# Layer 3's second mix: second half of the features first, later tokens first, and the next weights' contraction swapped to match

## The chip, the cores and the metric

The kernel runs on one NeuronCore of a Trainium2 chip. What counts is the device time of one execution in microseconds (us). The kernel before was run three times: 2449.55, 2449.95 and 2450.09 us, a median of 2449.95 us.

## What is computed

The input `x` has 128 graphs of 64 nodes with 256 features (8192 tokens), and all graphs share one 64 x 64 adjacency `adj`. Four layers follow one another, each added to `x`: a graph convolution with LSTMs over windows of nodes, masked attention, a graph convolution with batch normalisation, and layer 3, which this case is about. All of it is fp32. Layer 3, cut to what matters:

```python
def _slconv(x, adj, S, W):                 # here S is adj too
    support = jnp.einsum('bnf,fh->bnh', x, W)
    return jnp.einsum('nm,bmh->bnh', adj * S, support)
h = jnp.maximum(_layernorm(x), 0.0)
h = relu(_slconv(h, adj, adj, W1))         # 256 -> 512 features
h = relu(_slconv(h, adj, adj, W2))         # 512 -> 1024
x = x + _slconv(h, adj, adj, W3)           # 1024 -> 256
```

Mixing over nodes and multiplying with weights can be exchanged, so the kernel does for each group of tokens: mix, W1, Relu, mix, W2, Relu, W3, mix, add.

## The kernel before

**Groups.** The tokens are cut into 16 groups (`NG`) of 512 (`GN`), each of 4 token tiles (`GT`) of 128 tokens, which are two graphs. Layer 3 is one loop over `g` from 0 to 16 (lines 1571 to 1614). A pass issues, in program order: `first_weights` of group g; `last_mix` (k = 0) of group g - 1; `second_mix` of group g; `last_mix` (k = 1) and `finish` of group g - 1; `second_weights` of g; `start` (layer norm and first mix) of g + 1; `third_weights` of g. In group 0 there is no `last_mix`, and other matmuls (transposes back to tokens, line 1301) stand in that place.

**The order of the work.** The kernel is written in a framework whose planner puts each engine's instructions in order, by program order and by its own reckoning of what is ready, and sets the waits. Each engine then works through its queue in that order. `issue_after` adds an order within an engine. PSUM tiles are all taken from one pool of eight banks (`bank`, line 49).

**Mix** (line 132). It multiplies by the 64 x 64 matrix `w2s`. For two feature chunks of 128 at a time (`c0`, `c0 + 1`) and each token tile `t` it does 8 matmuls on 64 x 64 quarters of the array (line 144), with the activations as the stationary operand. Each is two records in the profile[...]. The results lie in two banks, one for each graph of a tile; a copy on VectorE and one on ScalarE (line 154) bring them to SBUF. The second mix has four chunks: chunks 0 and 1 with all four tiles, then chunks 2 and 3.

**The weights as seven products.** Every multiplication with weights is cut into 2 x 2 blocks and done as seven block products in place of eight (`seven`, line 170; `sevens`, line 241). The products 1, 5, 6 and 7 come first, into four banks in this order. ScalarE copies 1 and 5 to SBUF (lines 179 and 180), VectorE adds 6 and 7 to them (182 and 183). Then `finish`:
- Block (1,1) is summed on GpSimd from SBUF (line 187); its Relu is on ScalarE (line 237).
- Product 2 goes into the first bank; block (0,0) is its Relu (line 234).
- Product 3 goes into the second bank; block (0,1) is a sum on VectorE (line 193), then a Relu (237).
- Product 4 goes into the fourth bank; block (1,0) is a sum on VectorE (line 197), then a Relu (237).

In `first_weights` (line 1408, matmuls at 1418) a block (m, n) holds the tokens of tiles 2m and 2m + 1 and the feature chunks 2n and 2n + 1. Its last block, (1,0), is handled in two parts, one for each token tile (`parts` of line 1429).

**Second weights** (line 1438, matmuls at 1454). Blocks of the mixed activations `m1`: `act[c][n]` has chunks 2c and 2c + 1 and half n of the token columns. `differences` makes four combinations of them on VectorE (line 214). The weights' blocks `a2` and sums `s2s` are made once, on GpSimd, in `layer3_weights` (line 1154).

**Last mix and finish** (lines 1517 and 1530). `last_mix` does 4 matmuls for each k into two banks `pss`; `finish` adds the banks to `x` on VectorE (line 1542) and sends `x` out.

Of the kernel before, what the change touches and what calls it, by code (L numbers as in the profile page):

```python
# [9 lines left out]
AF = mybir.ActivationFunctionType  # L10
# [4 lines left out]
P = 128  # L15
D = 256
NODES = 64
NTOK = 8192
GT = 4
GN = GT * P  # L20
NG = NTOK // GN
# [17 lines left out]
def adj_preln_kernel(ctx: ExitStack, tc: tile.TileContext, x_in, adj, vec, bg0, bg1,  # L39
# [9 lines left out]
    def bank(shape=(P, 512)):  # L49
        return psp.tile(list(shape), F32, tag="ps", name="ps")  # L50
# [22 lines left out]
    w2s = const.tile([P, NODES], F32, tag="w2s", name="w2s")  # L73
# [55 lines left out]
                )  # L129
        return pss  # L130

    def mix(src, a2, chunks, dst, copies, swap=False, banks=None, behind=lambda t, last: None):

        for c0 in range(0, chunks, 2):
            pss = banks or [bank((P, 2, GT, NODES)) for _ in range(2)]
            for t in range(GT):
                for c in range(2):
                    for half in range(2):  # L140
                        for b in range(2):
                            rows = slice(b * 64, b * 64 + 64)
                            col = (c0 + c) * P + half * 64
                            last = nc.tensor.matmul(  # L144
                                pss[b][half * 64 : half * 64 + 64, c, t, :],
                                lhsT=src[rows, t, col : col + 64],
                                rhs=a2[rows, :],
                                start=True, stop=True,
                            )
                behind(t, last.ins)  # L150
            for b in range(2):
                if swap:
                    to = dst[:, c0 : c0 + 2, :].rearrange("p c (k b m) -> p b c k m", b=2, m=P)
                    last = copies[b](to[:, b], pss[b].rearrange("p c (k q) n -> p c k (q n)", q=2))
                else:
                    to = dst[:, c0 : c0 + 2, :].rearrange("p c (t b n) -> p b c t n", b=2, n=NODES)
                    last = copies[b](to[:, b], pss[b])
        return last.ins

    on_vector, on_scalar = nc.vector.tensor_copy, nc.scalar.copy  # L160
# [993 lines left out]
    def layer3_weights():  # L1154

        w31_tile = arena(keep)
        w31 = w31_tile[:, 0:2, :]
        nc.sync.dma_start(out=w31, in_=l3w1.rearrange("(c p) f -> p c f", p=P))  # L1160
        w32 = [arena(ar_left), arena(ar_left)]
        w32_view = l3w2.rearrange("(c p) (k f) -> k p c f", p=P, k=2)
        for k in range(2):
            nc.sync.dma_start(out=w32[k], in_=w32_view[k])
        w33 = arena(ar_left).rearrange("p a (b f) -> p (a b) f", f=D)
        nc.sync.dma_start(out=w33, in_=l3w3.rearrange("(c p) f -> p c f", p=P))
        a2 = [[w32[m][:, 2 * c : 2 * c + 2, :] for c in range(2)] for m in range(2)]
        s2s = [t[:, i : i + 2, :] for t in (arena(ar_left), arena(ar_left)) for i in (0, 2)]
        sums(nc.gpsimd, *a2[0], *a2[1], *s2s)
        nc.gpsimd.tensor_scalar(a2[1][1], a2[1][1], -1.0, None, ALU.mult)  # L1170
        b1 = [[w31[:, c, n * D : (n + 1) * D] for n in range(2)] for c in range(2)]
        t1s = [w31_tile[:, 2 + i // 2, (i % 2) * D : (i % 2 + 1) * D] for i in range(4)]
        differences(nc.gpsimd, *b1[0], *b1[1], *t1s, negate=True)
        b3 = [[w33[:, 4 * c : 4 * c + 4, n * P : (n + 1) * P] for n in range(2)] for c in range(2)]

        t3s = [t[:, i, :].rearrange("p (c f) -> p c f", c=4) for t in (a2[1][0], w1) for i in range(2)]
        differences(nc.gpsimd, *b3[0], *b3[1], *t3s, negate=True)
        return b1, t1s, a2, s2s, b3, t3s
# [175 lines left out]
    def first_start():  # L1354

        a = arena(ar_left)
        h = a[:, 0:2, :].rearrange("p a (b d) -> p (a b) d", d=D)
        halves = [slice(k * HN, (k + 1) * HN) for k in range(2)]  # L1360
        pss = [[bank((P, 2, D)) for _ in range(2)] for _ in range(3)]
        mixes = [bank((P, 2, GT, NODES)) for _ in range(2)]

        def keep_busy(n, behind):

            with tc.issue_after(behind):
                for _ in range(n):
                    nc.tensor.matmul(
                        pss[0][0].rearrange("p t d -> p (t d)")[:, 0:D], lhsT=ident, rhs=b1[0][0],
                        start=True, stop=True,  # L1370
                    )

        for half in halves:
            normalize(0, half, [0])
        turn_back(0, pss[0], [0])
        for g in range(1, 3):
            normalize(g, chunks=[0])
            turn_back(g, pss[g], [0])
        for half in halves:
            normalize(0, half, [1])  # L1380
        for g in range(1, 3):
            normalize(g, chunks=[1], on_scalar=range(2))
        evicted(1)
        lns = []
        for k in range(2):
            two = slice(2 * k, 2 * k + 2)
            with tc.issue_after(lns[0][2]) if k else nullcontext():
                turn_back(0, pss[0], [1], [k])
                add_back(0, pss[0], [k])
                lns.append(ln_scale(xs[0][:, two], None, 2, True))  # L1390
        for g in range(1, 3):
            last = turn_back(g, pss[g], [1])
        keep_busy(4, last)
        with tc.issue_after(lns[1][2]):
            add_back(1, pss[1], [0])
        for k in range(2):
            two = slice(2 * k, 2 * k + 2)
            rstd, nmr, _ = lns[k]
            applied = ln_apply(xs[0][:, two], h[:, two], rstd, nmr, 2, (1,) if k else ())
        with tc.issue_after(applied):  # L1400
            add_back(1, pss[1], [1])
        mix(
            h, w2s, 2, a[:, 2:4, :], (on_vector, on_scalar), banks=mixes,
            behind=lambda t, last: keep_busy(t % 2, last),
        )
        return a, lambda: add_back(2, pss[2])

    def first_weights(a, room):

        h1 = arena(ar_left)  # L1410
        act = [[a[:, 2 + c, m * HN : (m + 1) * HN] for c in range(2)] for m in range(2)]
        ss = [a[:, i // 2, (i % 2) * HN : (i % 2 + 1) * HN] for i in range(4)]
        summed = sums(nc.vector, *act[0], *act[1], *ss)

        def product(w, b):
            def issue(ps, first):
                for t in range(2):
                    nc.tensor.matmul(  # L1418
                        ps[:, t, :], lhsT=w[:, t * P : (t + 1) * P], rhs=b,
                        start=first and t == 0, stop=True, skip_group_check=True,  # L1420
                    )

            return issue

        p1, p5 = (room[:, i, :].rearrange("p (t f) -> p t f", t=2) for i in (2, 3))
        blocks = [[h1[:, 2 * m : 2 * m + 2, n * D : (n + 1) * D] for n in range(2)] for m in range(2)]
        seven(
            sevens((*act, ss), (*b1, t1s), product), [bank((P, 2, D)) for _ in range(4)], p1, p5,
            blocks, ends_in(blocks, AF.Relu), lambda b: [b[:, t] for t in range(2)],
        )()  # L1430
        return h1, summed

    def second_mix(h1, m1):


        mix(h1, w2s, 4, m1, (on_vector, on_scalar), swap=True)

    def second_weights(m1, room):

        h2 = [arena(ar_right) for _ in range(2)]  # L1440
        act = [
            [m1[:, 2 * c : 2 * c + 2, n * HN : (n + 1) * HN] for n in range(2)] for c in range(2)
        ]
        tt = arena(ar_right).rearrange("p i (c n) -> p i c n", c=2)
        ts = [tt[:, i] for i in range(4)]
# [125 lines left out]
    for g in range(NG + 1):  # L1571
        if g == 0:
            bring(0, 3)
        if g < NG:

            m1 = arena(ar_right)
            h1, summed = first_weights(a, m1)
            if g == 0:
                with tc.issue_after(summed):
                    finish_start()  # L1580
            if g == 0:
                bring(3, 2)
        if s3 is not None:
            pss = [bank((P, 2, D)) for _ in range(2)]
            if g == NG:
                pss = [pss, [bank((P, 2, D)) for _ in range(2)]]
            last_mix(pss[0] if g == NG else pss, s3, 0)
        if g < NG:
            second_mix(h1, m1)
            if g == 0:  # L1590

                later = [(b, [bank((P, 2, D)) for _ in range(2)]) for b in range(brought, ready)]
                for b, pss in later:
                    turn_back(b, pss)
                brought = ready
                bring(0, 1)
# [70 lines left out]
```

## Time and profile before

| What | Value |
|---|---|
| median of three runs | 2449.95 us |
| the profiled execution, its own time | 2449.65 us |
| its span, first to last instruction | 2447.9 us |
| TensorE matmuls busy (PE) | 2428.1 us (99%) |
| weight loads busy (PEld, beside PE) | 2072.4 us (85%) |
| VectorE / ScalarE / GpSimd busy | 1540.7 / 1127.7 / 464.0 us |
| granted TensorE clock | 1.0 |
| a pass of layer 3's loop, from one `last_mix` to the next (groups 10 to 11) | 47.60 us |

The profile is that of one execution. PE is TensorE's matmuls, PEld its weight loads, DVE VectorE, ACT ScalarE, POOL GpSimd, SP SyncE; L144 is line 144 of the kernel. A row of the timeline gives start and length in us, engine, line, operation, the tiles written and read, their shape, the number of records, and in brackets the idle time before the row and what ended it. Starts of matmuls are recorded; their ends are modelled.

### The profile page before, as it was taken

To read this page: it belongs to the slowest core of one execution; us is meant where nothing else is said; L and a number is where in the kernel's file an instruction comes from. 1 tells how busy PE (TensorE), PEld (TensorE's weight loads), DVE (VectorE), ACT (ScalarE), POOL (GpSimd) and SP (SyncE) were. 2 spreads that over 40 slices of the span, in tenths; PEclk is the share of its full clock that TensorE was granted. 3 is DMA by queue.
4 is the path that set the end of the run, shared out by engine and by line. 5 is a ranking of instruction groups with operands and counts; after the bars stand their busy time and mean duration, and the time that the engine had idled before them with its cause. 6 is when DMAs were issued, how large, how long until landed. Compare 5 with 4: busy or idle time off the path is not lost.

```text
span 2447.9 us, 46580 instructions
## 1 busy us (share of the span) xinstructions
PE 2428.1 (99%) x19564; PEld 2072.4 (85%) x19564; DVE 1540.7 (63%) x2768; ACT 1127.7 (46%) x2026; POOL 464.0 (19%) x400
## 2 busy tenths in 40 slices
PE   9999999999999999999999999999999999999999
PEld 6678888889999998888888864487988898898888
DVE  6668866656566575575699886476555445454544
ACT  4557754544445344353455566564333323323332
POOL 4432211111111111112234331023111111111110
PEclk9999999999999999999999999999999999999999
DMA  3200000001000000153246410010233100000000
GB/s 128 94 2 1 1 18 1 1 1 35 1 1 1 1 1 1 18 99 70 47 80 127 79 35 2 1 61 10 36 53 62 27 10 19 10 10 10 18 10 18
DMA packets 161586, 73.20 MB, mean 30 GB/s; under 512 B 104416, under 2 KB 157792, under 8 KB 161376
## 3 DMA queue, kind: packets, MB, share of 16 engines
q1 hardware_dynamic: 147712, 56.82, 9.4%
q0 software_dynamic: 12672, 12.58, 3.5%
q8 instruction: 154, 2.52, 0.4%
q10 hardware_dynamic: 992, 0.82, 0.1%
q14 instruction: 56, 0.46, 0.1%
HBM read 40.84 MB, written 20.97 MB: 25 GB/s over the span
## 4 chain that ended last, share of the span: by engine, by line
PE 90%; DVE 6%; ACT 2%; POOL 1%; issue 1%; DVEq 0%; POOLq 0%; ACTq 0%
PE ps L568 41%; PE ps L1454 16%; PE ps L1502 8%; PE ps L830 4%; PE ps L144 4%; PE ps L880 3%; PE ps L1418 2%; PE ps L511 2%; PE ps L487 2%; PE ps L1210 2%; PE ps L1261 2%; PE ps L902 1%; ACT arena L237 1%; POOL arena L187 1%; PE ps L963 1%
## 5 line engine op out<-in xcount | busy, mean ns | idle before, releaser
L568 PE MATMUL ps<-diff,s 128*128 128x256 f32 (+1 forms) x1824 | 393.5, 371 | 0.9 <-DVE diff L689 0.9
L1454 PE MATMUL ps<-arena 128*128 128x256 f32 x1792 | 392.6, 381 | 0.2 <-PE ps L1454 0.2
L1454 PEld LDWEIGHTS ps<-arena 128*128 128x128 f32 x1792 | 337.9, 190 | 54.3 <-issue 9.0
L568 PEld LDWEIGHTS ps<-diff,s 128*128 128x128 f32 x1824 | 345.9, 190 | 33.8 <-issue 1.6
L582 ACT ACTIVATE gates<-gates,lbias 128x512 f32<-128x512 f32 (+5 forms) x426 | 244.2, 620 | 200.5 <-DVE gates L193 144.4
L187 POOL TENSOR_TENSOR gates<-p 128x512 f32<-128x512 f32 (+1 forms) x115 | 148.9, 1294 | 881.8 <-DVE p L183 830.9
L568 PE MATMUL ps<-h,w 128*128 128x256 f32 (+1 forms) x1028 | 241.0, 371 | 0.0
L568 PE MATMUL ps<-diff,w 128*128 128x256 f32 (+1 forms) x1040 | 238.7, 370 | 0.0
L568 PEld LDWEIGHTS ps<-diff,w 128*128 128x128 f32 x1040 | 197.4, 190 | 18.2
L568 PEld LDWEIGHTS ps<-h,w 128*128 128x128 f32 x1028 | 195.0, 190 | 19.2 <-issue 0.5
L582 ACT ACTIVATE gates<-ps,lbias 128x256 f32<-128x256 f32 (+3 forms) x213 | 91.8, 477 | 247.6 <-PE ps L568 247.4
L187 POOL TENSOR_TENSOR arena<-arena 128x256 f32<-128x256 f32 (+1 forms) x73 | 81.9, 1121 | 579.9 <-DVE arena L183 550.2
L237 ACT ACTIVATE arena<-arena 128x512 f32<-128x512 f32 (+1 forms) x160 | 88.6, 582 | 187.2 <-POOL arena L187 95.0
L1502 PE MATMUL ps<-arena 128*128 128x128 f32 x1280 | 149.7, 276 | 0.0
L193 DVE TENSOR_TENSOR gates<-p,ps 128x512 f32<-128x512 f32 (+1 forms) x115 | 76.3, 663 | 114.5 <-PE ps L568 114.2
L1502 PEld LDWEIGHTS ps<-arena 128*128 128x128 f32 x1280 | 145.5, 192 | 1.1
L193 DVE TENSOR_TENSOR arena<-arena,ps 128x256 f32<-128x256 f32 (+1 forms) x73 | 43.6, 597 | 156.2 <-PE ps L1454 87.4
L568 PE MATMUL ps<-state,w 128*128 128x256 f32 (+1 forms) x512 | 116.1, 370 | 0.9 <-ACT p L179 0.8
L182 DVE TENSOR_TENSOR p<-p,ps 128x512 f32<-128x512 f32 (+1 forms) x131 | 86.8, 662 | 47.9 <-PE ps L568 46.8
L197 DVE TENSOR_TENSOR gates<-p,ps 128x512 f32<-128x512 f32 (+1 forms) x115 | 76.6, 666 | 63.3 <-PE ps L568 62.7
L568 PE MATMUL ps<-state,s 128*128 128x256 f32 (+1 forms) x512 | 115.8, 369 | 0.0
L830 PE MATMUL ps<-arena,w 128*128 128x512 f32 x256 | 114.3, 599 | 0.0
(207 smaller groups left out, 4020.9 us busy)
## 6 DMA issues: line engine op xcount, KB each, us to landing
x<-in_x SPq DMA_DIRECT2D x19, 512.0 KB, 4.6
y<-turned SPq DMA_DIRECT2D x64, 128.0 KB, 3.8
v<-vt SPq DMA_DIRECT2D x128, 64.0 KB, 2.1
w<-in_wih SPq DMA_DIRECT2D x4, 1024.0 KB, 8.1
x_for_h<-in_x SPq DMA_DIRECT2D x8, 512.0 KB, 6.8
x<-y POOLq DMA_DIRECT2D x8, 512.0 KB, 6.3
x_for_h<-y POOLq DMA_DIRECT2D x8, 512.0 KB, 6.7
z<-w SPq DMA_DIRECT2D x64, 64.0 KB, 2.0
```

The costliest lines, as they stand in the source:

```text
L144: last = nc.tensor.matmul(pss[b][half * 64 : half * 64 + 64, c, t, :], lhsT=src[rows, t, col : col + 64], rhs=a2[rows, :], start=True, sto ...
L182: nc.vector.tensor_tensor(p1, p1, ps[2], ALU.add)
L187: nc.gpsimd.tensor_tensor(out=out[1][1], in0=p1, in1=p5, op=ALU.add).ins
L193: nc.vector.tensor_tensor(out[0][1], p1, ps[1], ALU.add)
L197: last = nc.vector.tensor_tensor(to, p, q, ALU.add)
L237: nc.scalar.activation(o, o, func)
L568: nc.tensor.matmul(ps[:, r], lhsT=wc[:, j, :], rhs=bc, start=first and r == 0 and c == 0, stop=True, skip_group_check=True,)
L582: nc.scalar.activation(o, ps, func, bias=lbias[:, col : col + 1])
L830: nc.tensor.matmul(ps, lhsT=w1[:, c, m * P : (m + 1) * P], rhs=a[:, 2 + c, :], start=(c == 0), stop=(c == 1),)
L880: nc.tensor.matmul(ps[:, r, :], lhsT=w[:, r * P : (r + 1) * P], rhs=x, start=first and r == 0, stop=True, skip_group_check=True,)
L1454: nc.tensor.matmul(ps[:, r, :], lhsT=w[:, c, col : col + P], rhs=b[:, c, :], start=first and r == 0 and c == 0, stop=c == 1, skip_group_ch ...
L1502: nc.tensor.matmul(ps[:, t, :], lhsT=w[:, c, t * P : (t + 1) * P], rhs=b[:, c, :], start=first and t == 0 and c == 0, stop=c == 3, skip_gr ...
```

## The change

`mix` can be given an order: pairs of a first chunk and the token tiles in order. The second mix uses it: chunks 2 and 3 first, with the tiles 2, 3, 0, 1; then chunks 0 and 1 with the tiles 0 to 3. So that the chunks mixed first are contracted first, the blocks of `m1` and those of the second weights are exchanged along the contraction. The first weights' block (1,0) is no longer handled in two parts. The four banks of the second mix are taken ahead of the two of the last mix.

```diff
-    def mix(src, a2, chunks, dst, copies, swap=False, banks=None, behind=lambda t, last: None):
+    def mix(src, a2, chunks, dst, copies, swap=False, banks=None, behind=lambda t, last: None,
+            order=None):
...
-        for c0 in range(0, chunks, 2):
-            pss = banks or [bank((P, 2, GT, NODES)) for _ in range(2)]
-            for t in range(GT):
+        for c0, tiles in order or [(c0, range(GT)) for c0 in range(0, chunks, 2)]:
+            pss = banks.pop(0) if banks else [bank((P, 2, GT, NODES)) for _ in range(2)]
+            for t in tiles:
...
-        a2 = [[w32[m][:, 2 * c : 2 * c + 2, :] for c in range(2)] for m in range(2)]
+        a2 = [[w32[m][:, 2 - 2 * c : 4 - 2 * c, :] for c in range(2)] for m in range(2)]
...
-            h, w2s, 2, a[:, 2:4, :], (on_vector, on_scalar), banks=mixes,
+            h, w2s, 2, a[:, 2:4, :], (on_vector, on_scalar), banks=[mixes],
...
-            blocks, ends_in(blocks, AF.Relu), lambda b: [b[:, t] for t in range(2)],
+            blocks, ends_in(blocks, AF.Relu),
         )()
         return h1, summed
 
-    def second_mix(h1, m1):
+    def second_mix(h1, m1, banks):
...
-        mix(h1, w2s, 4, m1, (on_vector, on_scalar), swap=True)
+        mix(
+            h1, w2s, 4, m1, (on_vector, on_scalar), swap=True, banks=banks,
+            order=[(2, (2, 3, 0, 1)), (0, range(GT))],
+        )
...
-            [m1[:, 2 * c : 2 * c + 2, n * HN : (n + 1) * HN] for n in range(2)] for c in range(2)
+            [m1[:, 2 - 2 * c : 4 - 2 * c, n * HN : (n + 1) * HN] for n in range(2)]
+            for c in range(2)
...
+        if g < NG:
+            mixes = [[bank((P, 2, GT, NODES)) for _ in range(2)] for _ in range(2)]
         if s3 is not None:
             pss = [bank((P, 2, D)) for _ in range(2)]
...
-            second_mix(h1, m1)
+            second_mix(h1, m1, mixes)
```

## The prediction

> **What bounds the kernel now.** I began with the page: busy time and the chain that ended last.
>
> ```profile
> span 2447.9 us, 46580 instructions
> PE 2428.1 (99%) x19564; PEld 2072.4 (85%) x19564; DVE 1540.7 (63%) x2768; ACT 1127.7 (46%) x2026; POOL 464.0 (19%) x400
> PE 90%; DVE 6%; ACT 2%; POOL 1%; issue 1%; DVEq 0%; POOLq 0%; ACTq 0%
> ```
>
> TensorE sets the end; only what removes TensorE time or a hole in its queue can count. Next, the table by stretch over two passes of layer 3's loop (groups 10 and 11; a pass takes 47.60 us from about 1735 us on):
>
> ```profile
> 2164.40:2212.00 47.60, 47.49 (x461) 1.00 0.04 12
> 2212.00:2259.60 47.60, 47.50 (x461) 1.00 0.04 13
> ```
>
> TensorE has 0.10 us of plain idle time in a pass, so the changed stage must be read by start times. The timeline of group 10, TensorE and its weight loads (start, length, count, and in brackets the idle time before and who ended it):
>
> ```profile
> 2164.53 0.66 PE L1523 MATMUL ps<-arena,w2s 64*64 64x256 f32 x8
> 2165.01 2.45 PE L144 MATMUL ps<-w2s,arena 64*64 64x64 f32 x128
> 2167.28 0.61 PE L1523 MATMUL ps<-arena,w2s 64*64 64x256 f32 x8
> 2164.79 0.72 PEld L144 LDWEIGHTS ps<-w2s,arena 64*64 64x64 f32 x32
> 2165.76 0.57 PEld L144 LDWEIGHTS ps<-w2s,arena 64*64 64x64 f32 x28 [0.24 <-ACT arena L237]
> ```
>
> L144 is the second mix, 64 matmuls in 128 records; L1523 is the last mix of the group before. After 32 records (token tiles 0 and 1 of the first two feature chunks) the loads wait for a Relu on ACT. The chain of waits there:
>
> ```profile
> 2162.11 0.70 DVE arena L183
> 2162.95 1.28 POOL arena L187
> 2164.25 1.46 ACT arena L237 x3
> 2165.76 1.70 PE ps L144 x96
> ```
>
> The chain is DVE sum, POOL sum, then Relus queued one behind another on ACT. The timeline narrowed to ACT and to DVE gives each:
>
> ```profile
> 2164.25 0.63 ACT L237 ACTIVATE arena<-arena 128x512 f32<-128x512 f32 x1 [0.75 <-POOL arena L187]
> 2164.79 0.61 ACT L237 ACTIVATE arena<-arena 128x512 f32<-128x512 f32 x1
> 2165.30 0.40 ACT L237 ACTIVATE arena<-arena 128x256 f32<-128x256 f32 x1
> 2165.61 0.40 ACT L237 ACTIVATE arena<-arena 128x256 f32<-128x256 f32 x1
> 2163.83 0.69 DVE L193 TENSOR_TENSOR arena<-arena,ps 128x512 f32<-128x512 f32 x1 [1.02 <-PE ps L1418]
> 2164.63 0.42 DVE L197 TENSOR_TENSOR arena<-arena,ps 128x256 f32<-128x256 f32 x1
> ```
>
> These are, in order, the Relus of block (1,1) (later tokens, second features; POOL's), of (0,1), and of the two halves of (1,0). Block (0,0) was done at 2163.50 (L234). The mix wants (0,0), then (1,0), the **last** block made. Two other passes, groups 0 and 4:
>
> ```profile
> 1687.06 2.10 PE L144 MATMUL ps<-w2s,arena 64*64 64x64 f32 x128
> 1880.11 1.70 PE L144 MATMUL ps<-w2s,arena 64*64 64x64 f32 x96 [0.39 <-ACT arena L237]
> 1877.31 1.26 POOL L187 TENSOR_TENSOR arena<-arena 128x512 f32<-128x512 f32 x1 [7.11 <-DVE arena L183]
> ```
>
> In group 0 other matmuls fill the time and the mix runs through: 2.10 against 2.45 us. In group 4 POOL starts 0.29 us later than elsewhere and the wait is longer.
>
> **What the Trainium skill says.** "TensorE: Matmul & The Clock Gate", Step-by-step: weight loads may be pulled ahead of running matmuls, the matmuls stay in program order. The trace agrees: a mix's load at 2164.79, its matmul at 2165.01; after the wait both start within 2 ns, and everything behind stands still. "TensorEngine Tiling (Array Packing)", Key Properties: a change of tiling mode drains TensorE. It agrees: 0.309 us from the last L1418 start to the first L1523 start, against 0.216 in the stream; a cost that the change keeps. "Perfetto Trace Analysis", Tensor Engine Instruction: a matmul's end in the profile is estimated; hence I count from starts.
>
> **The change, part by part**, in us from the first L144 start (2165.008 in group 10; the other groups have the same offsets within 0.01, group 4 apart).
>
> *What a mix loses now.* Starts come four at a time every 0.0583. Without a wait, 32 fours would spread over 31 x 0.0583 + 0.02 = 1.83; they spread over 2.23 (2.45 less the 0.22 of the last). Lost, by the starts: 0.286 until token tile 2 starts, 0.048 until the pace is regained, then 0.025 + 0.048 for tile 3, whose half of the Relu is released separately: 0.407. Over groups 1 to 15: 14 times about 0.408 = 5.71, plus 0.70 in group 4: **6.41 us**. Group 0 loses nothing.
>
> *First quarter after* (tiles 2, 3; second features) reads (1,1). Its Relu ends at -0.129; from ACT's end to TensorE's load the trace shows 0.050, so -0.079. A load needs some 0.055 before its matmul can stream (loads follow each other by that after the wait), so -0.024, before the slot at 0. Cost 0, margin 0.02.
>
> *Second quarter* (tiles 0, 1) reads (0,1): Relu ends at 0.391, loaded by 0.391 + 0.050 + 0.055 = 0.496; the slot is 8 x 0.0583 = 0.466. Late by 0.03.
>
> *Third and fourth.* (0,0) is long done. (1,0) is now one DVE sum from -0.375 to 0.31 (0.69 in place of 0.42 + 0.41) and one Relu to about 1.0; the slot is 24 x 0.0583 = 1.40. Cost 0: three quarters of the mix cover it, with 0.3 to spare; without that cover today's 0.4 returns. ACT loses one instruction in a pass (0.63 for about 0.71), DVE one; neither bounds.
>
> *Banks.* The mix's four PSUM banks are now taken before the last mix's two. Counted as eight in turn (24 are taken in a pass, before and after), the last mix gets the first two banks of the first weights, freed by L234 and L193, in place of two long free. This **added wait**: L193 ends at -0.494, DVE to TensorE takes 0.053 in the trace, so -0.441 against -0.476 wanted: 0.035. Behind it stand L1523, the whole mix and the products. It and the second quarter's 0.03 don't add up: the later mix finds its block ready. The trace doesn't show which bank a tile has. If it is another long free one, the cost is 0; the other end is a rival below. I take 0.04 in a pass.
>
> *Copies and second weights.* The features mixed first are now those that the swapped weights contract first, so the first product and the first difference again wait for the first copies. The first two chunks end at 15 x 0.0583 + 0.02 + 0.22 = 1.11; the copies end near 1.86; the first L1454 matmul comes at 2.81 - 0.41 + 0.04 = 2.44. Slack 0.5, as before. Later DVE work keeps its distance from the mix's end, so a wait of 0.10 at the third product (its difference ends at 2171.255, the matmul starts at 2171.402) stays.
>
> *Setup.* The weights come in the same whole-tile loads, and POOL does the same sums on other halves: 0. No DMA, SP or POOL instruction passes another.
>
> *Group 4.* If POOL is late there again, the Relu ends at 0.160, the first quarter starts 0.26 late, the second block costs some 0.05 more: 0.32 lost in place of 0.70.
>
> **Sum**: 6.41 - 14 x 0.04 - 0.32 = **5.5 us** saved. Bounds: 6.1 with no wait left but group 4's; 4.7 if both small waits count and cost the 0.048 of regaining pace. The profiled execution took 2449.65 (span 2447.9, 1.75 around it): 2444.1. The median of the runs is 0.30 above it: **2444.4**.
>
> **Rivals.**
> - *More:* the second weights' third product no longer needs the last mix's bank, so the planner may put L1542's two DVE sums (2169.38 to 2170.66) behind the differences; the 0.10 goes too: 15 x 0.1 = 1.5, 2442.9. Against it: L1542 stays earlier in the program.
> - *The wait moves to the front:* (1,1) comes through POOL, the slowest step (1.28 us), with 0.02 to spare. Each 0.1 us that it is later takes 1.5 us of the gain. At 0.1 to 0.2 late 2.5 to 4 us remain: 2446 to 2447.5. For it: group 4. Against: nothing ahead of POOL's sum is changed.
> - *Nothing happens:* the planner puts the matmuls in another order by its own reckoning, or later work takes the time back: about 2450. Against: it kept program order in this stage, and TensorE's passes are full.
> - *Slower:* the last mix gets the bank that the first weights' fourth product used. Its reader is the (1,0) sum, now ending at 0.31; L1523 would wait from -0.48 to 0.36, or 0.84, and only the mix's 0.41 is saved: 15 x 0.43 = 6.5 slower, 2456.4. It decides from a release 0.4 us behind L1523's place. Against it: the count of banks.
>
> **How the numbers follow.** Forecast 0.66 (2443.8 to 2445.3), more 0.08, to the front 0.13, nothing 0.06, slower 0.07. A measurement of this kernel can tell about 0.2% (4.9 us) from no change; 0.61 of the forecast's 0.66 lies beyond it. Faster 0.61 + 0.08 = 0.69, same 0.05 + 0.13 + 0.06 = 0.24, slower 0.07. The range runs from 2442.8 (more) to 2446.8 (a good part of "to the front"); it leaves out nothing, slower and some of "to the front", under 0.2.
>
> **What would show it.** Right: L144's row with 128 records near 2.05 to 2.1 us and no wait for L237 after 32 records; passes of 47.23; one L197 of 128x512 in the first weights; L1523 up to 0.04 later behind L1418. Wrong: L144's first loads waiting for L237, L1523 waiting for L193 or L197 by over 0.1, L1454 starting with a wait for a copy, or passes still of 47.6.

## The result and the profile after

The changed kernel takes **2445.32 us** (median of 20 runs, 2444.55 to 2446.75), the kernel before 2449.88 us (20 runs beside it). The ratio is 0.9982 with a 95% interval of 0.9976 to 0.9988: 4.6 us saved, where 5.5 were forecast. The whole interval lies below 1, so the gain is real. The time stands at the slow edge of what the prediction calls its forecast (2443.8 to 2445.3), inside its wider range, and the gain is short of the 4.9 us that it thought likely (0.69) to be passed.

The profiled execution took 2446.36 us. The page, and the table by stretch over the passes of groups 10 and 11:

```profile
span 2444.5 us, 46563 instructions
PE 2425.3 (99%) x19564; PEld 2068.5 (85%) x19564; DVE 1539.8 (63%) x2752; ACT 1127.5 (46%) x2010; POOL 463.9 (19%) x400
PE 91%; DVE 5%; ACT 2%; issue 1%; DMA 0%; POOL 0%; DVEq 0%; ACTq 0%; POOLq 0%
```

```profile
2162.95:2210.23 47.28, 47.28 (x461) 1.00 0.04 12
2210.23:2257.51 47.28, 47.28 (x461) 1.00 0.04 13
```

TensorE stays the bound, and a pass is 0.32 us shorter (47.60 to 47.28). Fifteen passes make 4.8 us, yet the spans differ by only 3.4. The rest stands in the same table for a stretch long before layer 3; the figure behind the brackets is the granted TensorE clock:

```profile
1452.00:1453.50 1.50, 1.50 (x3) 0.57 0.06 11
1453.50:1457.50 4.00, 4.00 (x8) 0.73 0.01 2
```

In this execution the granted clock fell for some us: four matmuls there lost 0.34 to 0.42 us each, 1.6 us in all. Three of the ten profiles of this document have this fall at the same place (this kernel's, the one with the adds behind, the one with both edits), the others do not. It stands where both kernels do the same, so I compare passes, not spans. The change moves most line numbers (L144 is L145, L237 L238, L1454 L1459, L1523 L1528, L1542 L1547). The timeline of group 10 on TensorE and its loads:

```profile
2163.07 0.66 PE L1528 MATMUL ps<-arena,w2s 64*64 64x256 f32 x8
2163.56 2.07 PE L145 MATMUL ps<-w2s,arena 64*64 64x64 f32 x128
2163.47 2.01 PEld L145 LDWEIGHTS ps<-w2s,arena 64*64 64x64 f32 x128 [0.19 <-ACT arena L238]
```

The mix takes 2.07 us in place of 2.45, and its loads run through 128 records in place of stopping after 32. They still wait 0.19 us for ACT, at the front; but the matmul starts 0.483 us behind the last mix's first, exactly as before. The loads were 0.215 us ahead of the matmuls before and are 0.08 us ahead now, and that lost lead costs nothing here: read the matmul's start, not the load's idle time.

ACT and DVE, with the timeline narrowed to each: the Relus of (1,1), (0,1) and (1,0), and the sum of (1,0):

```profile
2162.79 0.63 ACT L238 ACTIVATE arena<-arena 128x512 f32<-128x512 f32 x1 [0.74 <-POOL arena L188]
2163.33 0.61 ACT L238 ACTIVATE arena<-arena 128x512 f32<-128x512 f32 x1
2163.90 0.63 ACT L238 ACTIVATE arena<-arena 128x512 f32<-128x512 f32 x1
2163.18 0.69 DVE L198 TENSOR_TENSOR arena<-arena,ps 128x512 f32<-128x512 f32 x1
```

From the mix's start (2163.56) the blocks leave ACT at -0.13, 0.39 and 0.98, as worked out; (1,0) is wanted at 1.40. The chain of waits of this stretch no longer leaves TensorE:

```profile
2157.10 6.05 PE ps L1419 x28
2163.14 0.59 PE ps L1528 x8
2163.74 1.89 PE ps L145 x128
2165.62 0.43 PE ps L1528 x8
2166.06 5.96 PE ps L1459 x26
```

Where a gain goes missing shows behind it, at the third product of the second weights. First the weight load there in the kernel before, then in the changed one:

```profile
2171.37 0.19 PEld L1454 LDWEIGHTS ps<-arena 128*128 128x128 f32 x1 [0.23 <-issue]
```

```profile
2169.60 0.19 PEld L1459 LDWEIGHTS ps<-arena 128*128 128x128 f32 x1 [0.29 <-issue]
```

"issue" hides a wait here: an instruction of its own on TensorE's sequencer waits for VectorE's third difference, which ends 0.147 us ahead of the matmul in both kernels. By starts, the step to this matmul is 0.295 us where it was 0.239, against 0.216 in the stream; the next step is 0.291 in both. So 0.056 us of each pass is given back.

### The profile page after: what moved, and what is told of

Read it like the earlier page. It is cut to its first block, busy times and chain, and to the rows that moved or that the text cites. A ratio compares the mean times of both kernels' runs of the same rounds, so it can differ in the third digit from the quotient of the medians.

```text
span 2444.5 us, 46563 instructions
## 1 busy us (share of the span) xinstructions
PE 2425.3 (99%) x19564; PEld 2068.5 (85%) x19564; DVE 1539.8 (63%) x2752; ACT 1127.5 (46%) x2010; POOL 463.9 (19%) x400
## 4 chain that ended last, share of the span: by engine, by line
PE 91%; DVE 5%; ACT 2%; issue 1%; DMA 0%; POOL 0%; DVEq 0%; ACTq 0%; POOLq 0%
PE ps L569 41%; PE ps L1459 16%; PE ps L1507 8%; PE ps L831 4%; PE ps L1419 4%; PE ps L145 4%; PE ps L881 3%; PE ps L512 2%; PE ps L488 2%; PE ps L1211 2%; PE ps L1262 2%; PE ps L903 1%; PE ps L1528 1%; PE ps L964 1%; DVE e L947 1%
## 5 line engine op out<-in xcount | busy, mean ns | idle before, releaser
L1459 PE MATMUL ps<-arena 128*128 128x256 f32 x1792 | 393.3, 380 | 0.3 <-DVE arena L215 0.3
L1459 PEld LDWEIGHTS ps<-arena 128*128 128x128 f32 x1792 | 337.9, 190 | 55.1 <-issue 9.8
L238 ACT ACTIVATE arena<-arena 128x512 f32<-128x512 f32 x144 | 88.1, 627 | 187.0 <-POOL arena L188 95.0
L194 DVE TENSOR_TENSOR gates<-p,ps 128x512 f32<-128x512 f32 (+1 forms) x115 | 76.4, 664 | 114.4 <-PE ps L569 114.2
L194 DVE TENSOR_TENSOR arena<-arena,ps 128x256 f32<-128x256 f32 (+1 forms) x73 | 43.6, 597 | 156.2 <-PE ps L1459 87.4
```

Source lines behind the costliest of these rows:

```text
L194: nc.vector.tensor_tensor(out[0][1], p1, ps[1], ALU.add)
L238: nc.scalar.activation(o, o, func)
L1459: nc.tensor.matmul(ps[:, r, :], lhsT=w[:, c, col : col + P], rhs=b[:, c, :], start=first and r == 0 and c == 0, stop=c == 1, skip_group_ch ...
```

## The experiments

The theory from the traces: the mix was paced by the order in which ACT lets the blocks out, and the new order takes that wait away. The 0.056 us comes from a wait that the prediction missed. In `first_weights`, `p1` and `p5` lie in chunks 2 and 3 of `m1`, the tile that the second mix's copies write. The chunks copied first were 0 and 1 and are now 2 and 3, so VectorE's first copy waits for TensorE, GpSimd and VectorE (by their semaphores, the counters with which engines wait for one another) in place of TensorE alone. VectorE's first copy in group 10, in the kernel before and in the changed one (the mix's last matmul starts at 2167.24 and 2165.41):

```profile
2166.58 0.69 DVE L154 COPY arena<-ps 128x512 f32<-128x512 f32 x1 [1.19 <-PE ps L144]
```

```profile
2164.80 0.69 DVE L155 COPY arena<-ps 128x512 f32<-128x512 f32 x1 [0.93 <-PE ps L145]
```

The rivals are in the expectations. Every kernel was run in rounds with the kernel before (2449.7 to 2449.8 us).

**The banks taken inside the mix again** (the changed kernel without the early banks):

```diff
-        if g < NG:
-            mixes = [[bank((P, 2, GT, NODES)) for _ in range(2)] for _ in range(2)]
...
-            second_mix(h1, m1, mixes)
+            second_mix(h1, m1, None)
```

> The changed kernel with the second mix's banks taken inside the mix again, behind the last mix's two; order of the mix, swap and single block (1,0) stay. Theory (the order of the mix is all that counts, the banks are free long before in both): 2445.3 us like the changed kernel, a mix spread over 1.85 us and no new wait. Rival (the banks taken early are what keeps the second mix or the third product from waiting): 15 passes with a wait of 0.1 us or more at L145's second half or at the third product of L1459, 2447 us or more.

Measured: 2444.99 us (ratio 0.9981, 0.9974 to 0.9988). The mix spreads over 1.85 us, L1528 starts 0.309 us behind L1419, and the third product's step is 0.291: as in the changed kernel within 0.01. The early banks do nothing for the time here.

**`p1` and `p5` out of the first copies' way** (the changed kernel with one index pair changed):

```diff
-        p1, p5 = (room[:, i, :].rearrange("p (t f) -> p t f", t=2) for i in (2, 3))
+        p1, p5 = (room[:, i, :].rearrange("p (t f) -> p t f", t=2) for i in (0, 1))
```

> The changed kernel with the first weights' copies p1 and p5 in chunks 0 and 1 of the mixed tile instead of 2 and 3. Theory (VectorE's first copy of the second mix now writes where p1 and p5 lay and waits for three engines in place of one, which starts it 0.055 us later against the mix's end, and the third product of the second weights pays for it): that copy starts 0.055 us earlier, the step to the third product shrinks from 0.295 to 0.24 us, 15 x 0.055 = 0.8 us, 2444.5 us. Rival (the third product is later because block (1,0) is one sum now): nothing changes, 2445.3 us.

Measured: 2444.24 us (0.9978, 0.9969 to 0.9986), 1.1 us below the changed kernel by the medians, 0.8 by the traces (table below). In the view of the copies' line, one entry is for the waits that VectorE's sequencer takes as instructions of their own (DVEq; count, then shortest, median and longest in ns). It is, in the kernel before, in the changed kernel and in this one:

```profile
L154 DVEq EVENT_SEMAPHORE  x15: 21/21/21, 1738.4 to 2405.5; - x15
```

```profile
L155 DVEq EVENT_SEMAPHORE  x15: 845/847/1154, 1737.7 to 2400.3; - x15
```

```profile
L155 DVEq EVENT_SEMAPHORE  x15: 21/21/21, 1738.5 to 2400.3; - x15
```

There are 15 in each, but in the changed kernel they stand ahead of the first copy and last until TensorE is done; here, as in the kernel before, they stand ahead of the second and find nothing to wait for. The first copy starts 1.194 us from the mix's start in place of 1.241, and the step to the third product is 0.238. The single sum of (1,0) is still there, so the rival falls.

**The last mix's adds behind the differences** (the changed kernel):

```diff
-            finish(g - 1, pss)
+            if g == NG:
+                finish(g - 1, pss)
         if g < NG:
             h2, behind = second_weights(m1, h1)
+            if s3 is not None:
+                with tc.issue_after(behind):
+                    finish(g - 1, pss)
```

> The changed kernel with the last mix's two adds to x put behind the four differences on VectorE. Theory (the third product waits for a difference that stands behind these two adds on VectorE; without them it is ready 1.2 us earlier): the step to the third product falls to 0.216 us and the next to 0.216 (0.155 us in a pass), 15 x 0.155 = 2.3 us, 2443.0 us. Rival (the adds then hold up the next group's layer norm or a bank, and the time comes back as a wait in L145 of the first mix or in the later products): 2445 us or more.

Measured: **2442.62 us** (0.9971, 0.9961 to 0.9982; 8 runs from 2442.0 to 2444.4). VectorE's timeline in group 10 has, in the changed kernel, the adds (L1547) ahead of the last two differences (L215):

```profile
2167.60 1.28 DVE L1547 TENSOR_TENSOR x_for_h<-x_for_h,ps 128x512 f32<-128x512 f32 x2
2168.80 1.41 DVE L215 TENSOR_TENSOR arena<-arena 128x512 f32<-128x512 f32 x2
```

With the adds behind:

```profile
2164.69 0.68 DVE L155 COPY arena<-ps 128x512 f32<-128x512 f32 x1
2165.48 2.02 DVE L215 TENSOR_TENSOR arena<-arena 128x512 f32<-128x512 f32 x3
2167.41 1.28 DVE L1547 TENSOR_TENSOR x_for_h<-x_for_h,ps 128x512 f32<-128x512 f32 x2
2168.61 1.40 DVE L92 BATCH_NORM_STATS2 st<-x_for_h 128x6 f32<-128x256 f32 x4
```

Both steps at the third product are 0.216, its weights' products spread over 24.062 us in place of 24.217, and the next group's statistics (L92) follow without harm.

**Both edits.**

> Both edits, p1 and p5 in chunks 0 and 1 and the two adds behind the differences. Theory (both work on the same wait, that of the third product, which is gone with either the larger one): 2443.0 us, the same as with the adds behind alone. Rival (the late copy costs something by itself, at the first product or elsewhere): another 0.8 us less, 2442.2 us.

Measured: 2442.63 us (0.9973, 0.9962 to 0.9984; 7 runs). Both steps at the third product are 0.216 here too, and layer 3 takes as long as with the adds behind alone (table below). The two don't add up: both work on one wait, and the late copy costs nothing elsewhere.

**The tokens in order** (the changed kernel):

```diff
-            order=[(2, (2, 3, 0, 1)), (0, range(GT))],
+            order=[(2, range(GT)), (0, range(GT))],
```

> The changed kernel with the token tiles of the first two chunks in the order 0, 1, 2, 3 in place of 2, 3, 0, 1. Theory (the mix is paced by the order in which ScalarE's queue lets the blocks out: (1,1) at -0.13, (0,1) at 0.39 us of the mix's natural start): TensorE waits for (0,1) ahead of the whole mix until 0.44, and 0.05 more until it is in pace, less the 0.025 of the second quarter: 0.46 us in a pass, 15 x 0.46 = 7 us, 2452 us. Rival (the gain comes from taking the second features first, the tokens don't matter): 2445.3 us.

Measured: 2452.09 us (1.0010, 1.0004 to 1.0017). TensorE's timeline shows the wait ahead of the mix, which starts 0.92 us behind L1528 where it started 0.48 behind:

```profile
2166.57 0.66 PE L1528 MATMUL ps<-arena,w2s 64*64 64x256 f32 x8
2167.50 1.69 PE L145 MATMUL ps<-w2s,arena 64*64 64x64 f32 x100 [0.26 <-ACT arena L238]
```

The new feature order with the old token order is slower than the kernel before: the gain needs both. (The new token order with the old feature order was not tried.)

**No swap in the second weights** (the changed kernel with the two index ranges as before):

```diff
-        a2 = [[w32[m][:, 2 - 2 * c : 4 - 2 * c, :] for c in range(2)] for m in range(2)]
+        a2 = [[w32[m][:, 2 * c : 2 * c + 2, :] for c in range(2)] for m in range(2)]
...
-            [m1[:, 2 - 2 * c : 4 - 2 * c, n * HN : (n + 1) * HN] for n in range(2)]
+            [m1[:, 2 * c : 2 * c + 2, n * HN : (n + 1) * HN] for n in range(2)]
```

> The changed kernel with the contraction of the second weights not swapped: their first blocks are chunks 0 and 1, which are mixed last now. Theory (the first product needs the first blocks' copies; without the swap these are the last ones, done near 2.8 us of the mix's start against 2.43 when TensorE gets there): L1459 begins some 0.45 us late in a pass, of which the third product's wait gives back about 0.1: 15 x 0.35 to 0.45 = 5 to 7 us, 2450.5 to 2452 us, no faster than the kernel before. Rival (the copies have slack enough, the swap is only for tidiness): 2445.3 us.

Measured: 2450.19 us (1.0001, 0.9993 to 1.0010), just under the theory's range. The second weights begin with a wait for the second copy, 1.107 us behind the mix's last start in place of 0.583:

```profile
2168.39 3.91 PE L1459 MATMUL ps<-arena 128*128 128x256 f32 x17 [0.45 <-DVE arena L155]
```

The third product then finds its difference ready (0.216), and a pass is 0.524 longer at one place and 0.185 shorter behind it. The order of the mix is worth nothing without the swap.

**Block (1,0) in one part, in the kernel before:**

```diff
-            blocks, ends_in(blocks, AF.Relu), lambda b: [b[:, t] for t in range(2)],
+            blocks, ends_in(blocks, AF.Relu),
```

> The kernel before with block (1,0) of the first weights handled as one sum and one Relu, the order of the mix as before. Theory (fewer instructions bring nothing by themselves; here they make the last block later): token tile 2 waits until the whole block is out at 1.03 us, where it waited until 0.75: a mix spread over some 2.44 us, 15 x 0.2 = 3 us slower than before, 2453 us. Rival (a good part of the gain comes from the two instructions fewer on VectorE and ScalarE in a pass): faster than before, 2447 to 2449 us.

Measured: 2452.78 us (1.0012, 1.0006 to 1.0019). Token tile 2 starts at 1.031 us where it started at 0.749, and the mix spreads over 2.440 us. So the two parts were what kept the old wait short, and their removal is no source of the gain.

**Block (1,0) in two parts, in the changed kernel:** the same edit the other way round.

> The changed kernel with block (1,0) in two parts again. Theory (the block is wanted at 1.35 us and is out at about 1.0 either way): 2445.3 us, no wait in the mix. Rival (the second part ends later and starts the copies late, or the single sum was what made the third product late): 0.8 us or more away from the changed kernel.

Measured: 2445.66 us (0.9983, 0.9977 to 0.9990), with a spread of 1.851 us and steps as in the changed kernel. With the new order the block has time enough either way.

**All kernels side by side.** The fall of the clock above comes in some executions and not in others, and so moves a median of few runs. So the table has beside it what one profile of each kernel shows of layer 3: from the first `last_mix` (in the pass of group 1) to the end, behind that fall.

| Kernel | Median, us | Layer 3 from group 1, us |
|---|---|---|
| before | 2449.88 | 712.5 |
| changed | 2445.32 | 707.6 |
| banks inside the mix | 2444.99 | 707.6 |
| `p1` and `p5` moved | 2444.24 | 706.8 |
| adds behind | 2442.62 | 704.9 |
| both | 2442.63 | 705.0 |
| tokens in order | 2452.09 | 714.6 |
| no swap | 2450.19 | 712.4 |
| before, one part | 2452.78 | 715.5 |
| changed, two parts | 2445.66 | 707.9 |

The two columns agree within 0.5 us on every comparison made above.

## Why the prediction was right, and where it was off

- **What the old mix lost (6.41 us): right.** The spread fell from 2.231 to 1.850 us in group 10; 1.83 was the floor. The two kernels that break one half of the order each (tokens, swap) lose the gain by the waits that were forecast, so the mechanism is shown.
- **First quarter, margin 0.02: right.** It costs nothing in any group but group 4.
- **Second quarter, late by 0.03: right.** It is 0.024: the first four matmuls start in time, the next four come 0.082 us behind them in place of 0.058.
- **The bank wait of 0.035: wrong, and harmless.** L1528 follows L1419 by 0.309 us in every kernel. In group 10 its first load starts 0.010 us behind the end of the sum L194, too soon to have waited for it (the prediction's step from VectorE to TensorE is 0.053). So it did not wait for that sum, and nothing shows a wait for any other bank; which bank it got, and how banks are given out, stays open. The slower rival, a wait for the (1,0) sum, did not happen either. The 0.04 a pass that was booked for this and the second quarter was 0.024: 0.2 us too much over 14 passes, which by luck hides a part of the next error.
- **Group 4: right.** POOL was late again. The mix started 0.23 us late there and spread over 1.931: 0.33 lost, 0.32 was forecast.
- **"Later DVE work keeps its distance from the mix's end, so a wait of 0.10 at the third product (...) stays": the step that failed.** VectorE's first copy starts 0.609 us ahead of the last mix matmul where it was 0.663, and the wait grew from 0.10 to 0.154. The prediction followed the copies by what they read and not by what they write over: `p1` and `p5` are named in the kernel. It cost 15 x 0.056 = 0.84 us, and moving `p1` and `p5` brought it back.
- **The sum.** 6.41 - 14 x 0.024 - 0.33 - 0.84 = 4.9 us, and the two profiles differ by 4.9 us over layer 3. The medians differ by 4.6; the 0.3 between the two is not explained. The prediction's lower bound of 4.7 had no room for the 0.84.
- **Of the rivals,** "more" named the right cause: it didn't happen by itself, but putting the adds behind the differences brought 2.7 us, by the medians and in the table. It took back the whole wait (15 x 0.154 = 2.3), where the prediction knew of 0.10; the rest is a single late start, below.

In each of the two profiles one pass has a third product that is 0.35 us later still, and not for the same reason. In the changed kernel (group 5) VectorE's second difference starts 0.46 us behind the second copy's end in place of 0.10. With the adds behind, the same difference is as late, but nobody waits for it any more: 2.3 + 0.35 is the 2.7. In the kernel before (group 3) the differences are on time and TensorE itself is late. GpSimd's late sum in group 4 is of this kind too: its sequencer was through with its wait at the usual time, and the sum began 0.3 us later than in other groups. What these three late starts wait for the traces don't show, and nothing was tried on them.

## What to carry to other kernels

When an engine eats blocks that several others make, write down when each block leaves the last queue, and take them in that order; then do the same for whoever eats what is made of them, or the wait only moves (the order without the swap gained nothing). Reordering writes also changes what each is written over: look up what lay in the first target, because the copy that waited for three engines started 0.054 us later than the one that waited for TensorE alone, though the other two were long done.

## What the runs showed of the hardware

- A second and third semaphore to wait for cost VectorE's copy about 0.054 us though they had been reached long before: it starts 0.106 us behind the modelled end of the last matmul of its chunks, and 0.052 with one to wait for (the kernel before, and the one with `p1` and `p5` moved). The wait becomes an instruction of its own on the sequencer. Where that instruction found nothing to wait for (21 ns), no cost showed. Whether two semaphores cost as much as three was not tried.
- TensorE shows the same. A weight load that waits by itself starts 0.050 us behind the end of a ScalarE instruction and 0.053 behind one of VectorE; where the wait is an instruction of its own on the sequencer, as at the third product and at the first product of the kernel without the swap, it starts 0.115 to 0.117 us behind VectorE's end.
- After a wait in mid-mix TensorE needs one step more to regain its pace: 0.106 us to the second four, 0.058 from there on, in both waits of groups 1 to 15 of the kernel before. The same 0.106 stands at the front of a mix whose loads were not ahead: in group 0, and in every pass of the kernel with the tokens in order.
